# Two-layer cross attention on one core: first loads moved to GpSimd's queue, softmax factors asked for one period later, weight sums spread over the first units

## The chip, the cores and the metric

One Trainium2 chip, one core of it. The metric is the device time of one execution in microseconds (us). An engine that computes is TensorE (PE; its weight loads are listed as PEld), VectorE (DVE), ScalarE (ACT) or GpSimd (POOL); SyncE (SP) issues DMAs. The DMAs that an engine issues stand in its instruction stream in order: when one has to wait for a semaphore, everything behind it on that engine waits too.

## The reference

Two attention layers, one after the other, on x (8 sequences of 100 positions, 640 wide, 20 heads of 32). The context has 722 tokens, 1024 wide: 77 text tokens and 645 others ("ip"). Text and ip have a softmax each.

```python
# layer 0, per sequence
q = x @ Wq.T
k, v       = text @ Wk.T, text @ Wv.T        # 77 tokens
k_ip, v_ip = ip @ Wk_ip.T, ip @ Wv_ip.T      # 645 tokens
x = (softmax(q k^T / sqrt(32)) v + softmax(q k_ip^T / sqrt(32)) v_ip) @ Wo.T + bo + x
# layer 1: the same with other weights, but
#   ip scores get an addend shared by the heads, 0.5 * sem, where
#   sem = (softmax(q k_text^T * scale over all channels) @ text) @ ip^T * scale
#   ip probabilities are multiplied by a mask over the 100 positions
```

## The kernel before, in words

All arithmetic is fp32. The work has three stages.

**First stage, to about 215 us.** Text products, sums of weight quarters, and q of layer 0. The large products of ip with the weights are made by a twice nested scheme of seven products for eight, so weights and activations are first added and subtracted: among others by `text_differences` (L1012, on VectorE; its instructions are L1018 and L1022), `operand_sums` (L895) and `last_operands` (L931) on GpSimd, which also stores the results to scratch memory in DRAM (`op_d`, `os_d`, `ol_d`, `tx_d`).

**First two units, to about 545 us.** `made` (L1069) is the list of the tasks of production units 0 and 1 (k and v of the first sequences). While it runs, the sums that later weights need are put between its tasks: `place(at, each, parts)` puts part i behind task at + each*i. The buffers of this stage come from a pool of its own; pools of the next stage (k, v, tail, p, one) lie in the same memory, so the first load into a tile of theirs has to wait until what lay there is done with. Among that are the operands that `last_operands` stores: L948 adds, L949 is the store (ol_d<-olv, issued by GpSimd).

**Main loop, to the end.** 80 "products" (u, c): 16 units u (8 sequences in each of two layers) by 5 column chunks c of four heads. In period n the loop makes the scores of product n, and finishes product n-1 (`last`):

| place in the period | what is asked for |
|---|---|
| start | scores(n, part 0): 512 tokens, into the two score banks sc0, sc1 (L1310 on) |
| 0 to 0.4 | tasks of production and small pieces (`between`) |
| then | transposes(n-1, j=0, 1) |
| 0.4 to 0.6 | tasks |
| then | transposes(n-1, j=2, 3), directly followed by scores(n, part 1): the last 133 ip tokens and the text, into the same two banks |
| 0.6 to 0.8 | tasks (from n = 74 on these come behind the next line) |
| then | transposes(n-1, j=4, 5) |
| 0.8 to 1.0 | tasks |
| end | values(n-1), the product with v |

Layer 0 is n = 0 to 39, layer 1 n = 40 to 79. Transposes (L1432) go to a bank and are copied out to `pt`, by ScalarE for j = 0, 2, 4, 5 (L1440), by VectorE for j = 1, 3 (L1442).

**Softmax steps and the list `later`.** `scores` asks for the first pair of maxima at once and puts the rest on the list `later`, each with a mark that says whether it reads the score banks: maxima(1), exponentials(0), exponentials(1); for part 1 also text maxima and differences, text exponentials, then `factors` (VectorE, L1365: L1367 to L1371) and `widened`, `scaled_rest` (GpSimd L1377; ScalarE L1388; VectorE L1383). In layer 0 the maxima (L1321) and the exponentials (L1335) read the banks. In layer 1 one VectorE instruction per head (L1327) writes scores plus addend to `p` in on-chip memory and takes the extreme; the exponentials then read `p`, not the bank. Text exponentials are L1357 (layer 1, one for four heads) and L1360 (layer 0). `next_task` takes one entry off `later` whenever at least 1.0 us of task time has gone by; `free_scores` (L1296) asks for all entries up to the last one with the mark; `emit(len(later))` for all. The transposes j = 4, 5 need `scaled_rest` and `wide`; values need all copies.

**What sets the order.** Instructions of TensorE, VectorE and ScalarE run in exactly the order in which the program asks for them (`tc.manual_schedule(engines=PINNED)`, L1571). SP's and GpSimd's are placed by a scheduler. Streamed weights (`w`, six buffers) are loaded ahead by `take` on SP (L329, L348). The loads of the attention (`load_q` L1103, `load_vt` L1109, `load_k` L1116, `load_v` L1124, `load_res` L1144) are all on SP.

Of the kernel before, what the change touches and what calls it, by code (L numbers as in the profile page):

```python
# [14 lines left out]
P = 128  # L15
# [4 lines left out]
NT = 77  # L20
NI = 645
NL = NI - 5 * P
# [21 lines left out]
ORDER = [(u, c) for u in range(NU - 2) for c in range(NC_)]  # L44
# [5 lines left out]
def two_layer_xattn(  # L50
# [681 lines left out]
    with ExitStack() as es:  # L732
# [306 lines left out]
        with tc.manual_schedule(engines=PINNED):  # L1039
            text_sums()  # L1040
            all_of(weight_sums("k", 2 * P))
            fifth_sums()
            text_k(0)
            load_wk(wkt[1])
            left_v(0)
            all_of(operand_sums("v", 0))
            v = weight_sums("v", HC)
            all_of(v[:2])
            load_operands("k", 0, nc.gpsimd)
            text_v(0)  # L1050
            all_of(v[2:])
            all_of(operand_sums("k", 0))
            text_v_blocks(0)
            load_wv(wvt[1])
            all_of(weight_sums("k", 2 * P))
            load_operands("v", 1, nc.gpsimd)
            text_k(1)
            for h in range(2):
                load_a(0, 0, h)
            v = weight_sums("v", HC)  # L1060
            all_of(v[:2])
            text_v(1)
            all_of(v[2:])
            text_v_blocks(1)
            all_of(operand_sums("v", 1))
            for h in range(2):
                load_a(0, 1, h)
            left_text()
            made = lapped(unit_tasks(0, nc.vector) + unit_tasks(1, nc.vector))  # L1069
            made.pop(0)[1]()  # L1070
            for kc in range(HK):
                outer_piece(0, 5, kc)
            for which in (5, 6, 7, 3):
                inner_sum(0, OUTER[0], which, nc.vector)
            aside = {}

            def place(at, each, parts):
                for i, g in enumerate(parts):
                    aside.setdefault(at + each * i, []).append(g)

            place(100, 1, [lambda: load_operands("k", 1, nc.gpsimd)])
            place(40, 6, text_differences())
            place(270, 10, last_operands())
            for x, (_, f) in enumerate(made):
                f()
                if x == 110:
                    place(120, 18, operand_sums("k", 1))
                all_of(aside.get(x, []))

    banks[:] = [(ps_b, "b")]  # L1090
# [12 lines left out]
    def load_q(u):  # L1103
        l, b = divmod(u, B)
        t = tpool.tile([P, NC_, S], F32, tag="q", name=f"q_{u}")
        nc.sync.dma_start(t, q_d[l][b // 2][:, b % 2])
        qs_[u] = t

    def load_vt(u):  # L1109
        l, b = divmod(u, B)  # L1110
        t = tpool.tile([NTAIL, C], F32, tag="vt", name=f"vt_{u}")
        nc.sync.dma_start(t[:NL], vl_d[l][b * NL : (b + 1) * NL, :])
        nc.sync.dma_start(t[NL:], vt_d[l][b * NT : (b + 1) * NT, :])
        vts[u] = t

    def load_k(u, c):  # L1116

        l, b = divmod(u, B)
        t = kpool.tile([P, NK], F32, tag="k", name=f"k_{u}_{c}")
        nc.sync.dma_start(t[:, :NI], k_d[u][:, c, :])  # L1120
        nc.sync.dma_start(t[:, NI:], kt_d[l][c][:, b * NT : (b + 1) * NT])
        ks[u, c] = t

    def load_v(u, c):  # L1124
        t = vpool.tile([P, NB, P], F32, tag="v", name=f"v_{u}_{c}")
        nc.sync.dma_start(t, v_d[u].rearrange("(j p) n -> p j n", p=P)[:, :, c * P : (c + 1) * P])
        vs[u, c] = t

    def load_sem(u):
# [162 lines left out]
    def emit(n):  # L1292
        for _ in range(n):
            later.pop(0)[1]()

    def free_scores():  # L1296

        emit(max([i + 1 for i, (r, _) in enumerate(later) if r], default=0))

    def scores(u, c, part):  # L1300
        k0, k1 = ((0, KA), (KA, NK))[part]
        if part == 0:
            pr[u, c] = ppool.tile([S, 4, NK], F32, tag="p", name=f"p_{u}_{c}")

            stats[u, c] = stat.tile([S, 11, 4], F32, tag="st", name=f"st_{u}_{c}")
        else:
            free_scores()

        scs = [ps_sc.tile([P, 2, 512], F32, tag=f"sc{h}", name=f"sc_{u}_{c}_{part}_{h}") for h in range(2)]
        for i in range(4):  # L1310
            rows = slice(32 * i, 32 * i + 32)
# [109 lines left out]

    def transposes(u, c, j, at_end=False):
        if j == 0:
            emit(len(later))
            pts[u, c] = one.tile([P, 6, 4 * S], F32, tag="pt", name=f"pt_{u}_{c}")
        rows = P if j < 5 else NTAIL
        if at_end and j in (2, 3):
            ps = ps_sc.tile([P, 2, 512], F32, tag=f"sc{j - 2}", name=f"pspt_{u}_{c}_{j}")[:, 0]
        else:
            ps = ps_b.tile([P, 512], F32, tag="b", name=f"pspt_{u}_{c}_{j}")  # L1430
        for i in range(4):
            nc.tensor.transpose(  # L1432
                ps[:rows, i * S : (i + 1) * S], pr[u, c][:, i, j * P : j * P + rows], ident[:S, :S]
            )
        dst, src = pts[u, c][:rows, j, :], ps[:rows, : 4 * S]
        if j == 5:
            nc.tensor.transpose(ps[:, 4 * S : 5 * S], wide[u, c], ident[:S, :S])
            nc.scalar.copy(heads_sum(u, c), ps[:, 4 * S : 5 * S])
        if j in (0, 2, 4, 5):
            nc.scalar.copy(dst, src)  # L1440
        else:
            nc.vector.tensor_copy(dst, src)  # L1442
# [128 lines left out]
    with tc.manual_schedule(engines=PINNED):  # L1571
        todo = production()
        load_q(0)
        load_vt(0)
        load_k(0, 0)
        done = [0]
        since = [0.0]

        def next_task():

            if todo[done[0]][0]:
                if later and since[0] >= 1.0:
                    emit(1)
                    since[0] = 0.0
                since[0] += todo[done[0]][0]
            todo[done[0]][2]()
            done[0] += 1

        def make(until):
            while done[0] < len(todo) and todo[done[0]][1] < until:  # L1590
                next_task()

        mark = [0]

        def apart(until):

            while done[0] < len(todo) and todo[done[0]][1] < until and 1.7 > sum(
                t for t, _, _ in todo[mark[0] : done[0]]
            ):
                next_task()  # L1600
            while held_banks[0] > 1 and done[0] < len(todo) and todo[done[0]][1] < until + 0.1:
                next_task()
            mark[0] = done[0]

        def between(n, a, b, small):

            mark[0] = done[0]
            near = 0.7 if n < NC_ * LAST[0] + 2 else 0.1
            for i, (_, f) in enumerate(small):
                make(n + a + (b - a) * (i + 1) / (len(small) + 1))  # L1610
                apart(n + b + near)
                f()
            make(n + b)
            apart(n + b + near)

        make(0.0)
        last = None
        for n, (u, c) in enumerate(ORDER):
            at = small_work(n)
            loads(n)  # L1620
            scores(u, c, 0)
            if n == len(ORDER) - 1:
                load_v(*last)
                load_v(u, c)
            between(n, 0.0, 0.4, at[0])
            if last:
                transposes(*last, 0)
                transposes(*last, 1)
            between(n, 0.4, 0.6, at[1])
            if last:  # L1630
                transposes(*last, 2)
                transposes(*last, 3)
            scores(u, c, 1)
            if n == NC_ * LAST[0] - 1:
                load_q(LAST[1])
            few = n >= NC_ * LAST[0] + 4
            if not few:
                between(n, 0.6, 0.8, at[2])
            if n < len(ORDER) - 2:
                load_v(u, c)  # L1640
            if n + 1 < len(ORDER):
                load_k(*ORDER[n + 1])
            if last:
                transposes(*last, 4)
                transposes(*last, 5)
            if few:
                between(n, 0.6, 0.8, at[2])
            between(n, 0.8, 1.0, at[3])

            emit(len(later) - (n == len(ORDER) - 1))  # L1650
            if last:
                values(*last)
            emit(len(later))
            last = (u, c)
        last_out(0, [NC_ - 1])
        for j in range(6):
            transposes(*last, j, at_end=True)
        last_out_add(0)
        values(*last)
        last_out(1, [NC_ - 1])  # L1660
        last_out_add(1)
# [46 lines left out]
```

## Time and profile before

| | |
|---|---|
| runs | 2091.28, 2091.79, 2104.17 us; median 2091.79 |
| profiled execution, its own time | 2102.3 us |
| its span, first to last instruction | 2100.5 us |
| mean granted TensorE clock | 0.979 |
| VectorE, ScalarE, GpSimd busy | 59%, 39%, 50% |
| instructions | 43283 |
| a layer 0 period | about 22 us |
| a layer 1 period | about 16.6 us; the last ten 10 to 12 us |

How to read it. The page lists busy times per engine, then the span in 40 slices of 52.5 us with a digit for tenths. "PEclk" is the TensorE clock that was granted, in tenths of full speed. A group row gives line, engine, operation, output<-input with shapes, count, busy us, mean ns of one, then idle time ahead of it and what ended that. A wait row reads "engine tile line <- what it waited for: us in total, times, longest". A timeline row is start (us), duration, engine, line, operation; in brackets the idle time ahead of it and its cause. A window row is the window, its length, busy us and counts of PE, PEld, DVE, ACT, POOL, then granted clock, DMA share and GB/s. SPq is SP's queue of DMAs.

### The profile page before, as it was taken

Reading aid. Unit: us, or ns where it says so; the run is one execution under the profiler, and the core shown is the slowest. Engines: PE = TensorE matmul, PEld = TensorE weight load, DVE = VectorE, ACT = ScalarE, POOL = GpSimd, SP = SyncE. Lnnn points to the kernel's source line nnn. Section 1 sums busy time; section 2 is a strip of 40 time slices with the busy share of each in tenths; the row PEclk is TensorE's granted clock in tenths of the full one; section 3 lists DMA queues with packets and bytes.
Section 4 is the critical chain, followed back from the end, with each engine's and each line's share of the span. In section 5 each row is a group of like instructions: output and inputs, shape, how many; then the busy total and the mean of one; then the engine's idle time right before and its main releaser. Section 6 shows DMA issues by size and latency. Waiting matters only on the chain. (4 is left out here: it accounts for less than half of the span.)

```text
span 2100.5 us, 43283 instructions
## 1 busy us (share of the span) xinstructions
PE 1971.8 (94%) x15422; PEld 1608.4 (77%) x15422; DVE 1231.7 (59%) x3047; ACT 829.0 (39%) x2839; POOL 1039.9 (50%) x1256
## 2 busy tenths in 40 slices
PE   9999876899999999999999999999999999999998
PEld 8676765787777788778788888887877777676787
DVE  2322673554655754665457666657676666766666
ACT  1001000010244443544354435445554555556665
POOL 2788887545456452644445674663455355210110
PEclk9999998999999999999999999999999999999999
DMA  9577887777666667766776676666766666554441
GB/s 350 204 264 262 263 278 231 199 215 213 201 183 197 201 178 205 212 189 181 204 226 197 205 216 205 202 204 177 211 187 200 178 200 194 149 159 119 137 132 53
DMA packets 439600, 419.13 MB, mean 200 GB/s; under 512 B 67691, under 2 KB 381819, under 8 KB 439131
## 3 DMA queue, kind: packets, MB, share of 16 engines
q1 hardware_dynamic: 407982, 306.67, 50.7%
q0 software_dynamic: 26400, 101.03, 13.4%
q10 hardware_dynamic: 5004, 8.68, 1.1%
q8 instruction: 124, 2.03, 0.4%
q14 instruction: 90, 0.73, 0.1%
HBM read 315.07 MB, written 101.18 MB: 198 GB/s over the span
## 5 line engine op out<-in xcount | busy, mean ns | idle before, releaser
L441 POOL TENSOR_TENSOR cv<-cv,cv 128x320 f32<-128x320 f32 x252 | 219.7, 897 | 305.0 <-DVE cv L179 280.3
L1440 ACT COPY pt<-pspt 128x400 f32<-128x400 f32 x320 | 156.1, 491 | 226.2 <-PE pspt L1432 225.5
L441 POOL TENSOR_TENSOR ck<-ck,ck 128x256 f32<-128x256 f32 (+1 forms) x252 | 201.0, 803 | 67.9 <-DVE ck L179 44.4
L1432 PE MATMUL pspt<-ident,p 100*128 100x100 f32 (+1 forms) x1920 | 210.1, 252 | 19.3 <-ACT pt L1440 7.1
L1432 PEld LDWEIGHTS pspt<-ident,p 100*128 100x128 f32 (+1 forms) x1920 | 189.4, 139 | 50.5 <-issue 14.9
L1335 ACT ACTIVATE p<-sc,st 100x512 f32<-100x512 f32 (+1 forms) x320 | 166.6, 533 | 71.5 <-DVE st L1342 49.2
L1335 ACT ACTIVATE p<-p,st 100x512 f32<-100x512 f32 (+1 forms) x320 | 177.1, 557 | 11.7 <-DVE st L1327 9.3
L1377 POOL COPY wide<-st 100x128 f32<-100x128 f32 x80 | 30.4, 380 | 292.8 <-DVE st L1371 265.2
L479 PE MATMUL psv_d<-w,i 128*128 128x160 f32 (+1 forms) x1008 | 170.0, 312 | 3.2 <-DMA w<-text_t 1.0
L479 PEld LDWEIGHTS psv_d<-w,i 128*128 128x128 f32 x1008 | 154.3, 193 | 14.8 <-issue 3.0
L176 ACT COPY cv<-psv_a 128x320 f32<-128x320 f32 x126 | 53.7, 426 | 262.6 <-PE psv_a L479 241.7
L1312 PE MATMUL sc<-k,q 32*100 32x210 f32 (+1 forms) x1280 | 149.2, 507 | 8.2 <-ACT p L1360 7.0
L176 ACT COPY ck<-psk_a 128x256 f32<-128x256 f32 (+1 forms) x126 | 47.2, 374 | 256.9 <-PE psk_a L525 209.1
L1388 ACT ACTIVATE p<-p,st 100x133 f32<-100x133 f32 x316 | 102.3, 395 | 115.5 <-DVE st L1371 115.4
L525 PE MATMUL psk_d<-i,w 128*128 128x256 f32 (+1 forms) x504 | 134.6, 390 | 10.6 <-DMA w<-op_dk 6.0
L1327 DVE CUSTOM_DVE_ANT_0 p<-sc,sem 100x512 f32<-100x512 f32 (+1 forms) x320 | 139.5, 489 | 1.3 <-PE sc L1312 1.3
L1442 DVE COPY pt<-pspt 128x400 f32<-128x400 f32 x160 | 91.6, 573 | 73.6 <-PE pspt L1432 72.7
L1321 DVE TENSOR_REDUCE st<-sc 100x2 f32<-100x1024 f32 (+1 forms) x160 | 126.6, 824 | 7.7 <-PE sc L1312 7.3
L525 PEld LDWEIGHTS psk_d<-i,w 128*128 128x128 f32 x504 | 92.5, 192 | 37.4 <-issue 16.2
L479 PE MATMUL psv_a<-w,a 128*128 128x160 f32 (+1 forms) x576 | 107.1, 330 | 5.2 <-DVE ck L179 5.0
L179 DVE TENSOR_TENSOR cv<-psv_d,cv 128x320 f32<-128x320 f32 x126 | 61.6, 489 | 82.0 <-PE psv_d L479 80.7
L479 PEld LDWEIGHTS psv_a<-w,a 128*128 128x128 f32 x576 | 93.7, 196 | 12.3 <-DVE ck L179 5.3
(278 smaller groups left out, 4409.6 us busy)
## 6 DMA issues: line engine op xcount, KB each, us to landing
w<-op_dv SPq DMA_DIRECT2D x252, 160.0 KB
a<-ip_t SPq DMA_DIRECT2D x33, 1024.0 KB
w<-op_dk SPq DMA_DIRECT2D x252, 128.0 KB
k<-k_d SPq DMA_DIRECT2D x80, 322.5 KB
v<-v_d SPq DMA_DIRECT2D x80, 320.0 KB
v_d<-cv POOLq DMA_DIRECT2D x28, 640.0 KB, 4.9
w<-os_dv SPq DMA_DIRECT2D x108, 160.0 KB
k_d<-ck POOLq DMA_DIRECT2D x28, 512.0 KB, 4.5
```

Source lines behind the costliest of these rows:

```text
L176: nc.scalar.copy(c11, flat(bank))
L441: nc.gpsimd.tensor_tensor(to[:, a, b], of[:, a, b], other[:, a, b], ALU.add)
L479: nc.tensor.matmul(ps[:, o * pitch : o * pitch + m], lhsT=of[:, kc, o * w : o * w + P], rhs=wt[:, kc, :], start=(o == 0 and kc == 0 and no ...
L525: nc.tensor.matmul(ps[:, : 2 * w], lhsT=wt[:, kc, :], rhs=of[:, kc, :], start=(kc == 0 and not go_on), stop=(kc == 1), skip_group_check=True,)
L1312: nc.tensor.matmul(scs[i // 2][:S, i % 2, : k1 - k0], lhsT=qs_[u][rows, c, :], rhs=ks[u, c][rows, k0:k1], start=True, stop=True)
L1321: nc.vector.tensor_reduce(st[:, part, 2 * h : 2 * h + 2], scs[h][:S, :, :n], AX.X, ALU.max, negate=True)
L1327: nc.vector.tensor_tensor_reduce(out=p[:, i, k0 : k0 + n], in0=scs[h][:S, i % 2, :n], in1=sems[u][:, k0 : k0 + n], scale=-1.0, scalar=3.0e ...
L1335: nc.scalar.activation(dst, dst if l else scs[h][:S, i % 2, :n], AF.Exp, bias=st[:, part, i : i + 1], scale=-1.0 if l else 1.0, accum_out= ...
L1388: nc.scalar.activation(p[:, i, KA:NI], p[:, i, KA:NI], AF.Copy, scale=mul[:, 1, i : i + 1])
L1432: nc.tensor.transpose(ps[:rows, i * S : (i + 1) * S], pr[u, c][:, i, j * P : j * P + rows], ident[:S, :S])
L1440: nc.scalar.copy(dst, src)
L1442: nc.vector.tensor_copy(dst, src)
```

## The change

Four edits. First, in the first two units `load_operands` for k of layer 1, the text differences, the last operands and the operand sums of k are placed at other tasks, for two of them at numbers that follow from the length of `made`. Second, q and vt of units 0 and 1, and k and v of unit 0's first two chunks, are loaded by GpSimd's queue instead of SP's. Third, `scores` calls `free_scores` for part 0 too, and `transposes` no longer asks for all of `later` at j = 0. Fourth, the end of a period asks only for what reads the score banks (in the last period, as before), so that factors and scaling of a product are left on the list for the next period.

```diff
-            place(100, 1, [lambda: load_operands("k", 1, nc.gpsimd)])
-            place(40, 6, text_differences())
-            place(270, 10, last_operands())
+            place(46, 1, [lambda: load_operands("k", 1, nc.gpsimd)])
+            place(16, 6, text_differences())
+            place(len(made) * 3 // 4, 8, last_operands())
             for x, (_, f) in enumerate(made):
                 f()
-                if x == 110:
-                    place(120, 18, operand_sums("k", 1))
+                if x == 50:
+                    place(60, (len(made) * 3 // 4 - 60) // 7, operand_sums("k", 1))
                 all_of(aside.get(x, []))
...
     def load_q(u):
...
-        nc.sync.dma_start(t, q_d[l][b // 2][:, b % 2])
+        queue = nc.gpsimd if u < 2 else nc.sync
+        queue.dma_start(t, q_d[l][b // 2][:, b % 2])
...
     def load_vt(u):
...
-        nc.sync.dma_start(t[:NL], vl_d[l][b * NL : (b + 1) * NL, :])
-        nc.sync.dma_start(t[NL:], vt_d[l][b * NT : (b + 1) * NT, :])
+        queue = nc.gpsimd if u < 2 else nc.sync
+        queue.dma_start(t[:NL], vl_d[l][b * NL : (b + 1) * NL, :])
+        queue.dma_start(t[NL:], vt_d[l][b * NT : (b + 1) * NT, :])
...
     def load_k(u, c):
...
-        nc.sync.dma_start(t[:, :NI], k_d[u][:, c, :])
-        nc.sync.dma_start(t[:, NI:], kt_d[l][c][:, b * NT : (b + 1) * NT])
+        queue = nc.sync if u or c > 1 else nc.gpsimd
+        queue.dma_start(t[:, :NI], k_d[u][:, c, :])
+        queue.dma_start(t[:, NI:], kt_d[l][c][:, b * NT : (b + 1) * NT])
...
     def load_v(u, c):
...
-        nc.sync.dma_start(t, v_d[u].rearrange("(j p) n -> p j n", p=P)[:, :, c * P : (c + 1) * P])
+        queue = nc.sync if u or c > 1 else nc.gpsimd
+        queue.dma_start(t, v_d[u].rearrange("(j p) n -> p j n", p=P)[:, :, c * P : (c + 1) * P])
...
     def scores(u, c, part):
...
             stats[u, c] = stat.tile([S, 11, 4], F32, tag="st", name=f"st_{u}_{c}")
-        else:
-            free_scores()
-
+        free_scores()
...
     def transposes(u, c, j, at_end=False):
         if j == 0:
-            emit(len(later))
             pts[u, c] = one.tile([P, 6, 4 * S], F32, tag="pt", name=f"pt_{u}_{c}")
...
-            emit(len(later) - (n == len(ORDER) - 1))
+            if n == len(ORDER) - 1:
+                emit(len(later) - 1)
+            else:
+                free_scores()
             if last:
                 values(*last)
-            emit(len(later))
+            if n == len(ORDER) - 1:
+                emit(len(later))
             last = (u, c)
```

## The prediction, made before the changed kernel ran

> **What bounds the kernel now.** I read the page's busy times first, then TensorE's waits and granted clock, then the groups kept apart by shape, then single periods of the timeline.
>
> ```profile
> PE 1971.8 (94%) x15422; PEld 1608.4 (77%) x15422; DVE 1231.7 (59%) x3047; ACT 829.0 (39%) x2839; POOL 1039.9 (50%) x1256
> PE   9999876899999999999999999999999999999998
> PEclk9999998999999999999999999999999999999999
> ```
>
> TensorE is busy 94% of the span, evenly but for slices 5 to 7 (about 210 to 370 us). A change can win little more than its idle time; it loses each microsecond that TensorE is kept waiting, so the question is who waits for whom after the new order. TensorE's waits, whole span:
>
> ```profile
> PE psv_e L479 <- DMA w<-op_dv: 22.5, 6, 15.2
> PE psv_a L479 <- DVE ck L179: 7.4, 5, 2.5
> PE pspt L1432 <- ACT pt L1440: 7.1, 8, 1.4
> PE sc L1312 <- ACT p L1360: 7.0, 5, 2.1
> ```
>
> The columns are total, times, longest. One wait of 15.2 us stands out (326.9 to 342.1 us). The rest are short: after 1434 us, where layer 1 begins, they sum to about 41 us. The score matmuls (sc), which need the two score banks free, wait next to nothing. Why not is seen in a layer 1 period:
>
> ```profile
> 1870.95 0.56 PE L1432 MATMUL pspt<-ident,p 100*128 100x100 f32 x4 [0.55 <-ACT pt L1440]
> 1871.06 0.49 ACT L1440 COPY pt<-pspt 128x400 f32<-128x400 f32 x1
> 1871.44 0.61 PE L1312 MATMUL sc<-k,q 32*100 32x210 f32 x8
> 1871.55 0.57 DVE L1442 COPY pt<-pspt 128x400 f32<-128x400 f32 x1 [1.77 <-PE pspt L1432]
> ```
>
> Scores part 1 start at 1871.44, directly behind transposes j=3: the readers of part 0 (maxima; in layer 0 exponentials too) finished long before, because the old program asks for all of `later` ahead of transposes j=0. VectorE's copy of j=3 ends at 1872.12, 0.69 after the scores began (1871.55+0.57-1871.44); ScalarE's copy of j=2 ends 0.11 after they began (1871.06+0.49-1871.44; in a layer 0 period at 713 us 0.26).
>
> **What the order of the changed program, built, says.** TensorE's order is the same. ACT and DVE run the same instructions in another order, pinned. With the emission at transposes j=0 gone, what tasks do not trickle out one per microsecond is forced out by `free_scores` directly ahead of scores part 1, thus behind the copies of j=2 (ACT) and j=3 (DVE). Counting over the 80 periods:
> - Layer 0, part 0's exponentials behind the j=2 copy: all four in 5 periods (in two of them maxima(1) too behind the j=3 copy), the last two in 6.
> - Layer 1, maxima(1) of part 0 behind the j=3 copy: in 21 periods with factors (L1367 to L1371) and L1383 of the product before in between, in 3 with L1383 alone, in 9 with only the copy, in 7 not.
>
> Scores part 1 use the same banks, so TensorE waits in these 44 periods.
>
> **Durations** (groups by shape):
>
> ```profile
> L1335 ACT ACTIVATE p<-sc,st 100x512 f32<-100x512 f32 x160 | 108.6, 690 | 22.0 <-DVE st L1321 22.0
> L1388 ACT ACTIVATE p<-p,st 100x133 f32<-100x133 f32 x316 | 102.3, 395 | 115.5 <-DVE st L1371 115.4
> L1327 DVE CUSTOM_DVE_ANT_0 p<-sc,sem 100x512 f32<-100x512 f32 x160 | 101.4, 684 | 0.6 <-PE sc L1312 0.6
> L1383 DVE TENSOR_TENSOR p<-p,st 100x308 f32<-100x308 f32 x80 | 41.8, 522 | 0.0
> ```
>
> They overlap a little; by pitch in the timeline an exponential takes 0.73 us, a pair of L1327 1.30, L1367 to L1371 with L1383 1.63 (L1383 0.47 of it beside its neighbour).
>
> **Emission, layer 0.** Four exponentials: 0.11 to 0.26 + 4 x 0.73, about 2.95 us (3.2 where maxima(1) are late too); two: about 1.5. Sum 2 x 3.2 + 3 x 2.95 + 6 x 1.5 = 24.3 us.
>
> **Emission, layer 1.** Copy ends at +0.69, then 1.63, then 1.30, 0.06 from the end of the read until TensorE goes on (as in the rows of 1995 us below); the second pair of score matmuls, which needs it, would have come 0.26 after the first: 0.69+1.63+1.30+0.06-0.26 = 3.42. With L1383 alone about 2.18, with neither 1.79. Sum 21 x 3.42 + 3 x 2.18 + 9 x 1.79 = 94.4. One period pays part of it already:
>
> ```profile
> 1995.44 0.60 PE L1312 MATMUL sc<-k,q 32*100 32x210 f32 x4 [0.54 <-DVE st L1327]
> 1996.66 0.60 PE L1312 MATMUL sc<-k,q 32*100 32x210 f32 x4 [0.62 <-DVE st L1327]
> ```
>
> There maxima(1) happen to be late and TensorE waits 1.2 us for them: the mechanism in the trace of before. 94.4 - 1.2 = 93.2.
>
> **The end.** From product 74 no task lies between scores part 1 and transposes 4. L1388 (four, 1.30) and part 0's exponentials (2.9) then stand on ScalarE ahead of copies 4 and 5, which the value matmuls need: about 1.5 us in each of 6 periods, 9; in three periods the previous text exponentials stand there as well, 1 us each. 12 us. Earlier in layer 1 the tasks behind part 1 cover the same (2 to 4 us of matmuls); without that cover it would be another 27 x 1.5 = 40.
>
> **The clock.** After the short wait above:
>
> ```profile
> 1992.26:1998.50 6.24, 5.08 (x44) 3.48 (x41) 6.10 (x27) 4.99 (x14) 0.41 (x1) 0.94 1.05 309
> 1997.70:2001.10 3.40, 3.40 (x19) 3.40 (x19) 2.06 (x14) 0.80 (x3) 0.00 (x0) 0.50 1.17 294
> ```
>
> The granted clock (third column from the end) is 0.50 for 3.4 us behind it. After 540 us the trace has 16 TensorE gaps of 1.6 us or more; 11 are followed by half clock, 47.8 us in all, 3.0 us per gap, so 1.5 us lost per gap. 44 x 1.5 = 66 us. Bounds: 0, and 6.8 us of half clock per gap (the longest after 540), 3.4 lost, 150.
>
> The Trainium skill, "TensorE: Matmul & The Clock Gate", section "HAM oscillation", speaks of idle gaps of more than about 3.4 us as what costs the clock; by that only the 21 longest could, some 32 us instead of 66. The trace has half clock after gaps of 1.63 to 2.5 us, so the measurement decides.
>
> **What comes back.** Of the 41 us of waits in layer 1 the other engines' lateness (DVE adds, copies) is caught up while TensorE waits: 25 taken, with 10 for their half clock (bounds 0, and 41 + 15). Layer 0's score waits of 7.0 us (for ACT's text exponentials at the period's end) shrink by 3. VectorE no longer stands at L1367:
>
> ```profile
> DVE st L1367 <- ACT p L1357: 44.9, 34, 3.9
> ```
>
> That is VectorE's time, not TensorE's, and its 59% share does not need it; it is contained in the 25.
>
> **The start.** SP stood 15.5 us at the first q load (L1106), whose memory needs the last store of ol_d, issued by GpSimd at 332.67. Behind it on SP was the weight load that TensorE waited for:
>
> ```profile
> SPq L1106 <- DMA ol_d<-olv: 15.5, 1, 15.5
> ```
>
> The 12 moved DMAs leave SP for GpSimd's queue. But in the built order load_res(0) (L1155) takes q's place on SP and waits for the same store. So the stall is only shortened, by as much as GpSimd reaches that store earlier: its last sums are asked for sooner, which drops waits of 4.6, 1.8 and 1.4 and one add of 0.8 ahead of it, while about 3.5 us of new waits appear: 5 us (bounds 0, and 15.2 + 6.8 for its half clock). GpSimd pays 12 issues at 0.54 to 0.80 us, 6.5 to 9.6 us, and the landing waits of v and k (1 and 5 us); it is idle 334 to 345 us, which hides them, and four cv tiles lie between it and TensorE. Uncovered they would cost at most the same 10 to 16 us once. The text differences (13.7 us of VectorE, L1018 and L1022, from 261 to 295 us) come some 30 us earlier, where VectorE is busy 48 of 65 us and TensorE waits little for it; I take 0, with 13.7 each way as bounds, the most that the block can delay or release. GpSimd's operand sums for k move likewise; TensorE's waits for those weights (w from op_dk, os_dk and o_d) sum to some 18 us from 215 to 545 us, the bound of a gain; a loss of the same size if GpSimd, busy 46 of 65 us there, comes as late elsewhere; again 0. The Trainium skill, "DMA: Bandwidth & Descriptors", section "Issuing engines are not separate DMA queues", says that spreading issues over engines saves issue time alone; no run here shows it.
>
> **Sum.** 24.3 + 93.2 + 12 = 129.5; clock +66; back -(25+10+3) and -5: +152. The profiled execution took 2102.3 us (span 2100.5), 10.5 above the median of 2091.8; added to the median: 2244 us.
>
> **Rivals.**
> - Stalls as counted, but the clock hardly falls and everything in layer 1 is caught up: 129.5 - 41 - 5 = +84, 2175. For it: 5 of 16 gaps cost no clock. Against: 11 did.
> - The clock falls harder, 3.4 us per gap: 129.5 + 150 - 43 = +236, 2328. For it: layer 1's periods are 16.6 us, so gaps come close together; against: after 540 us only three half-clock stretches of 6.8 us exist.
> - Faster: VectorE, freed from L1367's 44.9 us, is early at the adds that TensorE waits for (psv_a, psk_d and pspt on DVE, some 29 us in all) and their clock (10): -39, with the start -5: 2048. It decides only if fewer than about 8 periods (39 / (3.42 + 1.5)) have the late maxima; the built order has 33 in layer 1.
> - The change does not do what it says: SP's stall stays, as another load takes its place. Price 5 us of the sum, never its sign.
>
> **How the numbers follow.** Forecast 0.57; milder clock 0.22; harder clock 0.13; faster 0.05; within 1% (about what a measurement of this kernel can tell from no change) 0.03. The range takes the forecast and most of the two beside it: 2150 (milder, with half the end hidden, -6, and the start giving 22 instead of 5, -17: 2152) to 2310 (3 us lost per gap: 129.5 + 132 - 43 = +218). Slower by over 1%: 0.57+0.22+0.13 = 0.92.
>
> **What would show it.** PE sc L1312 <- DVE st L1327 at some 90 us over 30 or more times, and <- ACT p L1335 at some 20; PEclk digits of 8 and 9 in place of 9 in layer 1, half-clock stretches of 3.4 us behind the waits; L1367's wait for L1357 nearly gone; psv_e's wait for op_dv still about 10 us, SP waiting at L1155. Wrong if sc's waits stay under 40 us, or if TensorE's other waits vanish by more than 40.

## The result, and the profile after

| | before | after |
|---|---|---|
| median | 2093.36 us (4 runs, 2091.28 to 2104.17) | 2269.18 us (4 runs, 2265.14 to 2270.11) |
| ratio | | 1.0825, 95% interval 1.0785 to 1.0865 |
| span of the profiled execution | 2100.5 us | 2263.4 us |
| granted clock, mean | 0.979 | 0.947 |

The change makes the kernel 8% slower. Forecast were 2244 us, +152 on the median; measured are +176 between medians and +163 between the profiled executions. The page of the changed kernel first:

```profile
PE 2061.5 (91%) x15422; PEld 1668.8 (74%) x15422; DVE 1246.1 (55%) x3047; ACT 824.3 (36%) x2839; POOL 1040.2 (46%) x1268
PE   9999769989999998999999989999898998888887
PEclk9999989999999999999999999999898998888888
```

TensorE has the same 15422 instructions and is busy 89.7 us longer. Some 72 us of that is the clock: half of the time in which TensorE worked at half clock, a half that is 107.1 us after and 35.2 before. But for one in slice 6, the 8s among the clock's digits stand from slice 29 on, where layer 1 runs. Most of the rest is seen in the matmuls of scores part 1, before and after:

```profile
L1312 PE MATMUL sc<-k,q 32*100 32x210 f32 x640 | 51.1, 382 | 1.2 <-DVE st L1327 1.2
L1314 PE MATMUL sc<-k,q 32*100 32x210 f32 x640 | 85.2, 409 | 109.4 <-DVE st L1329 89.0 <-ACT p L1337 20.1
```

One of them takes 409 ns in place of 382, but together they keep TensorE busy 85.2 us in place of 51.1. All eight of a product overlap when they come together (0.61 us for x8 in the prediction's row at 1871.44); when a wait splits them, four alone take as long (0.60 us for x4 in the row at 2174.92 below).

The other 73 us of the span are idle time of TensorE. Its waits (total, times, longest) say for whom:

```profile
PE sc L1314 <- DVE st L1329: 89.0, 34, 3.8
PE sc L1314 <- ACT p L1337: 20.1, 18, 1.8
PE psv_e L479 <- DMA w<-op_dv: 12.2, 3, 8.0
PE psf L554 <- DMA w<-wki: 7.5, 5, 4.3
PE psk_d L525 <- DVE ck L179: 7.3, 4, 3.7
PE psk_a L525 <- DMA w<-os_dk: 7.1, 3, 3.3
PE sc L1314 <- ACT p L1362: 7.0, 5, 2.1
```

(L1329 and L1337 are L1327 and L1335 of before: the lines are 1 to 4 further on.) The scores, which waited 1.2 us for VectorE's maxima before, wait 89.0 us. One of these waits, in the timeline of the changed kernel:

```profile
2174.41 1.19 DVE L1443 COPY pt<-pspt 128x400 f32<-128x400 f32 x2 [0.33 <-PE pspt L1433]
2174.92 0.60 PE L1314 MATMUL sc<-k,q 32*100 32x210 f32 x4
2175.57 0.47 DVE L1369 TENSOR_REDUCE st<-p 100x4 f32<-100x308 f32 x1
...
2176.73 0.47 DVE L1385 TENSOR_TENSOR p<-p,st 100x308 f32<-100x308 f32 x1
...
2177.12 0.68 DVE L1329 CUSTOM_DVE_ANT_0 p<-sc,sem 100x512 f32<-100x512 f32 x1
...
2177.73 0.69 DVE L1329 CUSTOM_DVE_ANT_0 p<-sc,sem 100x512 f32<-100x512 f32 x1
...
2178.48 1.02 PE L1314 MATMUL sc<-k,q 32*100 32x210 f32 x4 [2.96 <-DVE st L1329]
```

VectorE copies transposes 1 and 3, then makes the factors of the product before, and only then reads the second score bank, which the second half of scores part 1 needs. Nothing of this is more work; it is the same work in an order that has TensorE's need last. The window rows of layer 1 up to product 73 and of the last six periods, first before, then after (granted clock is the third column from the end):

```profile
1445.20:2017.30 572.10, 536.48 (x5035) 429.09 (x5027) 384.39 (x1309) 316.21 (x1024) 195.91 (x236) 0.98 0.59 174
2017.30:2100.50 83.20, 74.37 (x898) 64.11 (x891) 54.74 (x213) 53.41 (x177) 7.84 (x14) 0.96 0.26 72
```

```profile
1477.70:2148.50 670.80, 589.54 (x5033) 467.70 (x5029) 398.50 (x1309) 316.44 (x1024) 195.95 (x236) 0.91 0.50 148
2148.50:2263.40 114.90, 89.79 (x895) 73.25 (x891) 55.85 (x213) 52.91 (x177) 7.86 (x14) 0.82 0.18 52
```

By stages, from the first score matmuls of a product to those of the next stage in the two traces ("clock lost" is half of the time at half clock in the stage):

| stage | before | after | more | more idle on TensorE | clock lost, before and after |
|---|---|---|---|---|---|
| to product 0 | 551.2 | 545.3 | -5.9 | -8.4 | 18.8, 17.1 |
| layer 0 | 894.0 | 932.4 | +38.4 | +19.6 | 10.2, 22.2 |
| layer 1, to product 73 | 572.1 | 670.8 | +98.7 | +45.6 | 11.9, 59.7 |
| the last six periods | 83.2 | 114.9 | +31.7 | +16.3 | 3.6, 20.6 |

### The profile page after: what moved, and what is told of

It reads as the page before. It is cut to its first block, busy times and chain, and to the rows that moved or that the text cites. A ratio compares the mean times of both kernels' runs of the same rounds, so it can differ in the third digit from the quotient of the medians.

```text
span 2263.4 us, 43383 instructions
## 1 busy us (share of the span) xinstructions
PE 2061.5 (91%) x15422; PEld 1668.8 (74%) x15422; DVE 1246.1 (55%) x3047; ACT 824.3 (36%) x2839; POOL 1040.2 (46%) x1268
## 5 line engine op out<-in xcount | busy, mean ns | idle before, releaser
L1314 PE MATMUL sc<-k,q 32*100 32x210 f32 (+1 forms) x1280 | 185.6, 532 | 116.3 <-DVE st L1329 89.0
L1433 PEld LDWEIGHTS pspt<-ident,p 100*128 100x128 f32 (+1 forms) x1920 | 199.3, 144 | 40.8 <-issue 20.4
L1433 PE MATMUL pspt<-ident,p 100*128 100x100 f32 (+1 forms) x1920 | 219.8, 259 | 6.7 <-DVE ck L179 5.7
L1337 ACT ACTIVATE p<-sc,st 100x512 f32<-100x512 f32 (+1 forms) x320 | 166.6, 533 | 49.8 <-DVE st L1344 43.5
L1314 PEld LDWEIGHTS sc<-k,q 32*100 32x100 f32 x1280 | 61.0, 169 | 159.5 <-DVE st L1329 101.0
L1337 ACT ACTIVATE p<-p,st 100x512 f32<-100x512 f32 (+1 forms) x320 | 176.5, 556 | 3.4 <-DVE st L1329 3.3
L479 PEld LDWEIGHTS psv_d<-w,i 128*128 128x128 f32 x1008 | 156.2, 195 | 16.3 <-issue 3.0
L1329 DVE CUSTOM_DVE_ANT_0 p<-sc,sem 100x512 f32<-100x512 f32 (+1 forms) x320 | 141.6, 489 | 33.3 <-PE sc L1314 33.2
```

Source lines behind the costliest of these rows:

```text
L479: nc.tensor.matmul(ps[:, o * pitch : o * pitch + m], lhsT=of[:, kc, o * w : o * w + P], rhs=wt[:, kc, :], start=(o == 0 and kc == 0 and no ...
L1314: nc.tensor.matmul(scs[i // 2][:S, i % 2, : k1 - k0], lhsT=qs_[u][rows, c, :], rhs=ks[u, c][rows, k0:k1], start=True, stop=True)
L1329: nc.vector.tensor_tensor_reduce(out=p[:, i, k0 : k0 + n], in0=scs[h][:S, i % 2, :n], in1=sems[u][:, k0 : k0 + n], scale=-1.0, scalar=3.0e ...
L1337: nc.scalar.activation(dst, dst if l else scs[h][:S, i % 2, :n], AF.Exp, bias=st[:, part, i : i + 1], scale=-1.0 if l else 1.0, accum_out= ...
L1433: nc.tensor.transpose(ps[:rows, i * S : (i + 1) * S], pr[u, c][:, i, j * P : j * P + rows], ident[:S, :S])
```

## The experiments

**The theory** (A): late readers of the score banks keep TensorE waiting, and the clock falls behind the waits. The rivals: the loads and the moved sums cost the time (B); the late factors and scaling cost it by themselves (C, G); the clock is low for another reason (E).

**Emission alone.** The kernel before with the third and fourth edit.

> The kernel before with the third and fourth edit alone (what is asked for when); loads and weight sums as before. Theory A (late readers of the score banks make TensorE wait, and the clock falls behind the waits): nearly the whole loss, 2265 to 2280 us, scores waiting about 89 us for maxima (the layer 1 instruction on VectorE) and about 20 us for exponentials. Rival B (the loads on GpSimd's queue and the moved sums cost time as well): under 2240, the rest being theirs.

Measured: 2263.43 us against 2092.86, ratio 1.0788 (1.0747 to 1.0828). The two score rows are those of the changed kernel, 89.0 and 20.1 us, to the tenth. The median lies 1.6 us under the expected band; the loss is all there, and B falls.

**The start alone.** The changed kernel with the old emission.

> The changed kernel with the emission of before: loads on GpSimd's queue and spread sums alone. Theory A: 2082 to 2092 us, since the first stage ended 6 us earlier in the changed kernel (551.2 to 545.3 us) and nothing later reads it. Rival B: over 2100.

Measured: 2092.31 us, ratio 0.9999 (0.998 to 1.0017). No loss, but no gain either: it lies 0.3 us above the band that A expected. SP still stands before the same store, now at the residual's load, and TensorE still waits at the same weight:

```profile
SPq L1159 <- DMA ol_d<-olv: 8.6, 1, 8.6
```

```profile
PE psv_e L479 <- DMA w<-op_dv: 15.4, 3, 12.3
```

**Bank readers first.** Factors still come a period later, but the readers of the banks are taken out of the list ahead of them.

```diff
+    def readers_only():
+        for e in [e for e in later if e[0]]:
+            later.remove(e)
+            e[1]()
...
     def scores(u, c, part):
...
-        free_scores()
+        (emit(len(later)) if part else free_scores())
...
     def transposes(u, c, j, at_end=False):
         if j == 0:
+            readers_only()
```

> The changed kernel, except that at transposes j=0 the entries that read the score banks are asked for, out of their order, and all that is left at scores part 1. Factors and scaling still come a period later. Theory A: the score waits are gone (under 10 us), clock back near 0.98, 2075 to 2100 us. Rival C (what costs is that factors and scaling come late: transposes 4 and 5 and the values wait for them): the time stays over 2200 us, with TensorE waiting at pspt and pv instead.

Measured: 2140.73 us, ratio 1.0208 (1.0172 to 1.0244): between the two. The waits for the maxima are gone (0.6 us are left). Most of what remains is C's, in one place: in the last six periods (114.0 us, against 83.3 with the start alone) TensorE waits at the transposes for the late scaling. The waits in those periods:

```profile
PE pspt L1439 <- ACT p L1395: 15.5, 6, 3.2
PE pspt L1439 <- ACT pt L1447: 2.1, 2, 1.2
```

Layer 1 up to product 73 takes 577.0 us, 3.9 more than with the start alone. There tasks lie between scores part 1 and transposes 4, and TensorE waits for the scaling only 5.7 us in 34 periods. Layer 0 takes 907.4 us, 19.3 more than with the start alone; why stays open.

**The same, with the old emission from product 73 on.** The edit, against the run before:

```diff
     def transposes(u, c, j, at_end=False):
         if j == 0:
-            readers_only()
+            (emit(len(later)) if ORDER.index((u, c)) >= 73 else readers_only())
...
+            elif n >= 73:
+                emit(len(later))
             else:
                 free_scores()
```

> The kernel that asks for the bank readers first, with the emission of before from product 73 on, where no task lies between scores part 1 and transposes 4. If its loss of 48 us sits there (TensorE waited 15.5 us at transposes for the late scaling in the last six periods, which took 31 us longer than before), 2105 to 2115 us; if the loss is spread over the loop, within 10 us of 2141.

Measured: 2108.93 us, ratio 1.0091 (1.0064 to 1.0119); the last six periods take 81.9 us. So 32 of the 48 us were the end's. Of the rest some 13 us stand in layer 0 (901.6 against 888.1 with the start alone), and were not followed further.

**Each of the two emission edits by itself.** First the one at j=0 (the period's end as before):

> The changed kernel with the end of a period as before (all is asked for there); only the emission at transposes j=0 is gone. Theory A, refined: the leftover factors fill the head of the list, so that the maxima behind them are not reached by the tasks. Without leftovers the order has late maxima in 3 periods in place of 33: 2095 to 2115 us (3 waits, and the last six periods with exponentials ahead of copies 4 and 5, 5 to 10 us). Rival F (the missing emission at j=0 is enough by itself): over 2200 us.

Measured: 2081.87 us, ratio 0.9958 (0.9934 to 0.9982). Better than expected: not a loss but a gain. Layer 1 up to product 73 takes 561.6 us, against 573.1 with the start alone. There TensorE no longer waits at transposes for copies (5.9 us for ScalarE's and 3.1 for VectorE's with the start alone, 0.2 now), which fits that copies 0 and 1 no longer stand behind a block of maxima and exponentials. F falls. Then the edit at the period's end, with j=0 kept:

> The changed kernel with the emission at transposes j=0 kept; only the end of a period leaves factors and scaling to the next one. Theory A, refined: no maxima behind copies, so 2085 to 2105 us. Rival G (leaving factors to the next period costs by itself): over 2120 us.

Measured: 2169.54 us, ratio 1.0378 (1.0355 to 1.0401). A's expectation failed and G's holds: leaving the factors over costs by itself, though no maxima stand behind copies. TensorE now waits for VectorE's copies themselves; before, the first of these rows had 5.0 us and the second did not occur:

```profile
PE pspt L1434 <- DVE pt L1444: 22.5, 19, 2.7
PE psv_a L479 <- DVE pt L1444: 15.2, 3, 6.0
```

Why is in the timeline of this kernel:

```profile
1546.38 0.46 DVE L1369 TENSOR_REDUCE st<-p 100x4 f32<-100x308 f32 x1
...
1549.06 0.46 DVE L1385 TENSOR_TENSOR p<-p,st 100x308 f32<-100x308 f32 x1
...
1549.45 0.68 DVE L1329 CUSTOM_DVE_ANT_0 p<-sc,sem 100x512 f32<-100x512 f32 x1
1550.06 0.68 DVE L1329 CUSTOM_DVE_ANT_0 p<-sc,sem 100x512 f32<-100x512 f32 x1
1550.67 0.56 DVE L1444 COPY pt<-pspt 128x400 f32<-128x400 f32 x1
...
1551.29 0.91 PE L1434 MATMUL pspt<-ident,p 100*128 100x100 f32 x8 [2.55 <-DVE pt L1444]
```

Factors and late maxima are one block of VectorE work (here 4.3 us, of which L1371 alone takes 1.22 us; its median is 0.16). Asked for at j=0 it stands ahead of copy 1, and the next transposes wait for their bank; asked for at scores part 1 it stands behind copy 3, and the scores wait. The block moves, and in these two places TensorE waits for it.

**The clock by itself.** 20 more transposes, whose results nobody reads, ahead of scores part 1 in the 21 periods with factors ahead of the maxima.

```diff
+            if n in (41, 42) or 60 <= n < 80 and n != 68:
+                for _ in range(20):
+                    nc.tensor.transpose(fill[0][:, 4 * S : 5 * S], pr[last][:, 0, : P], ident[:S, :S])
             scores(u, c, 1)
```

> The changed kernel with 20 more transposes (about 2.7 us of TensorE, results never read) ahead of scores part 1, in the 21 layer 1 periods in which factors stand ahead of the late maxima. TensorE works where it waited; the order on ACT and DVE is the same. Theory A, its clock part (half clock is paid for the idle gap): scores wait some 50 us less for the maxima, the clock rises, and the time falls by 30 to 55 us although nothing was taken away: 2215 to 2240 us. Rival E (the low clock has another cause, for instance what the other engines do, or it does not set the time there): within 10 us of 2269, or longer by part of the added work.

Measured: 2219.63 us against 2269.18 of the changed kernel (ratio to the kernel before 1.062, 1.0597 to 1.0642, where the changed kernel had 1.0825). TensorE does more and ends some 50 us earlier. Its waits for the maxima and the granted clock of the same two stages:

```profile
PE sc L1314 <- DVE st L1329: 33.7, 34, 3.6
```

```profile
1471.60:2109.00 637.40, 584.03 (x5331) 466.55 (x5327) 398.71 (x1309) 315.87 (x1024) 195.90 (x236) 0.97 0.52 156
2109.00:2215.90 106.90, 90.35 (x1017) 75.25 (x1011) 55.83 (x213) 52.96 (x177) 7.86 (x14) 0.95 0.20 56
```

0.91 has become 0.97 and 0.82 has become 0.95; after 540 us TensorE is at half clock for 87.1 us in place of 207.1, which is 60 us of time. Half clock is paid for the idle time, and E falls.

**A start that clears SP.** The start alone, with the loads that the scheduler would put in q's place on GpSimd's queue as well.

```diff
-            nc.sync.dma_start(t[:, :n], x_t[:, b : b + n])
+            queue = nc.sync if g else nc.gpsimd
+            queue.dma_start(t[:, :n], x_t[:, b : b + n])
```

(Likewise the first three tiles of output weights in load_wo, and load_sem and load_g of unit 8.)

> As the run with the start alone, and the further loads that the scheduler would put in q's place on SP (first residual, three output weights, the first text keys and text rows of layer 1) on GpSimd's queue too, so that SP waits for no memory of the first stage. Theory A's reading of the start (SP waits for the last store of the first stage's operands, whatever load stands there): psv_e's wait for op_dv of 8.0 us falls under 3 us, 2065 to 2085 us. Rival D (the weights that this wait holds back would be late anyway, or GpSimd's own work is delayed by the issues): no gain over the start alone, within 5 us.

Measured: 2085.19 us, ratio 0.9951 (0.9928 to 0.9974). The median lies 0.2 us above the band. SP waits for no store of ol_d any more. TensorE still waits 3.8 us at that place (up to 332.6 us; under 3 was expected) and then 3.0 us for another weight at 345 us: weights are late there for other reasons too. D falls, by 7 us against the start alone (the two intervals do not meet); the gain is a third of what the old wait of 15.2 us and its half clock might have given.

**A version that beats both.** The j=0 emission dropped up to product 72, everything else as before:

```diff
     def scores(u, c, part):
...
-        else:
-            free_scores()
-
+        free_scores()
...
     def transposes(u, c, j, at_end=False):
         if j == 0:
-            emit(len(later))
+            if ORDER.index((u, c)) >= 73:
+                emit(len(later))
```

> The kernel before, start and period end unchanged, with one edit: up to product 72 nothing is asked for at transposes j=0 (free_scores asks ahead of the scores instead). Theory A, refined by the run without j=0's emission (2082 us): the gain of that run is due to the exponentials and maxima no longer standing ahead of copies j=0 and j=1, so 2075 to 2085 us, its gain in layer 1. Rival H (that gain came from the start, the loads and sums): within 4 us of the kernel before.

Measured: 2082.86 us, ratio 0.995 (0.993 to 0.997); layer 1 up to product 73 takes 558.0 us, against 572.1 before. H falls. With the cleared start:

> The same edit together with the start in which GpSimd's queue also takes the first residual, the first three output weights and layer 1's first text loads (alone: 2085 us, 7.7 under before). If the two gains add, 2066 to 2076 us; if they overlap, 2077 to 2085 us.

Measured: 2072.37 us against 2095.01, ratio 0.9894 (0.9862 to 0.9926). The two gains add: 12.2 and 7.7 us alone, 22.6 together. This is the fastest kernel of the study.

## Why the prediction was right, point by point

- **Order and waits, layer 1**: right. Forecast 93.2 us in 33 periods; 89.0 us in 34 waits. The two are not quite the same measure. The forecast's 3.42 counts from where the second pair of score matmuls would have started, 0.26 us after the first; a wait counts from the end of the first pair, 0.60 us after its start. In the forecast's measure the wait shown above is 2.96 + 0.60 - 0.26 = 3.30, and the 34 waits are some 100 us. That a split pair also loses its overlap with the other is priced in the forecast only by this difference. (By the prediction's own terms its 2.18 would be 1.79 + 0.47 = 2.26, which is 0.2 us in the sum.)
- **Layer 0**: 24.3 us forecast, 20.1 measured (18 waits, since both banks can wait in a period). With the clock 24.3 + 11 x 1.5 - 3 = +38; measured +38.4. The agreement is in part luck: TensorE is idle 19.6 us longer and loses 12.0 us to the clock, and most of the rest is the score matmuls, which are busy 8.6 us longer there. The small term in the sum was wrong: the waits for ACT's text exponentials did not shrink by 3, they are 7.0 us in both kernels.
- **The clock**: the mechanism right, the term mis-sized. Forecast 66 us less 10 returned; measured 207.1 us at half clock after 540 us where it was 53.7, so (207.1 - 53.7) / 2 = 77 us. There are 40 gaps of 1.6 us and more, 16 before (forecast: 44 periods with waits), and 35 of them are followed by half clock. But each takes 207.1 / 40 = 5.2 us of it, where before it was 53.7 / 16 = 3.4 (4.7 against the forecast's 3.0, if only the stretches behind gaps are counted): half of the stretches are 6.8 us long, where before most were 3.4. The price was read off gaps of 2.7 us at most and put on waits of 3.42. It lies between the forecast and the rival with the harder clock. The rule weighed in the prediction (the Trainium skill, "TensorE: Matmul & The Clock Gate", section "HAM oscillation": idle gaps of more than about 3.4 us) is not what these traces show: the 40 gaps last 2.6 us on average and 3.8 at most, and 30 of the 35 that are shorter than 3.4 us are followed by half clock.
- **The end**: 12 us were counted twice. The likely reason: while TensorE waits for the late maxima, ScalarE gets through what stands ahead of copies 4 and 5: after the change TensorE waits 19.1 us for the maxima in those periods and 0.3 and 0.2 us at transposes and values. The term exists, but shows only when the score waits are taken away: 15.5 us in the run with the readers first. Forecast for the last six periods 6 x 3.42 + 12 + 6 x 1.5 = 41.5, measured 31.7.
- **What comes back**: 25 forecast. In layer 1 up to product 73 TensorE waits 69.9 us for the maxima, 68.7 more than before, and is idle only 45.6 us longer: 23.1 came back. (Layer 1's first scores are at 1445 us, not at 1434 as the prediction has it.)
- **VectorE's wait at L1367** (L1369 after): 44.9 us became 4.4, and TensorE got nothing for it, as forecast. The rival in which this decides is out.
- **The start**: 5 us forecast, the stage ended 5.9 us earlier, TensorE's wait 8.0 in place of 15.2 us. One execution says little here: over all traces that wait is 15.1 to 19.4 us in the three with the old start and 5.9 to 17.4 us, 10.3 on average, in the seven with the new one. So the forecast's 5 us show on average at that place, but in the time of the start alone they do not (0.998 to 1.0017). That SP's stall stays, because another load takes its place, was right.
- **Sum**: by stages -5.9 + 38.4 + 98.7 + 31.7 = +162.9 between the profiled executions. By kind they are 73.2 of idle time, 71.9 of clock while TensorE works, and 17.8 of busy time beyond that, near what the score matmuls lose by being split. The forecast's +152 is 56 of clock and 129.5 - 28 - 5 = 96.5 of all else, where 73.2 + 17.8 = 91.0 were measured. That the second part fits so well is in part luck: the end's 12 us counted twice and the lost overlap, which was not fully priced, offset each other. What is short is the clock.

What the prediction did not see is that the two emission edits have to be told apart: it spoke of the missing emission at j=0, which alone is a gain of 0.4%. The entries left over from the period before alone cost some 78 us. Together the two cost more, about 177 us: the entries left over stand at the head of the list, the tasks reach them first, and with no emission at j=0 the maxima behind them are forced out only at scores part 1.

## What to carry to other kernels

Work that is put off does not vanish from an in-order engine: ask which instruction of the bounding engine waits behind the place to which it moves, in each stage, and above all where the covering work is gone. When a list is emptied first in, first out, what is left over on it delays what is put on it next, so ask by need (who holds a bank that the next step wants), not by age. And a wait of 2 to 4 us on TensorE can cost more than its length: after 540 us the 40 gaps of this kernel are 105 us of idle time, and the half clock costs 104 us more.

## What the runs showed of the hardware that was not expected

- Longer idle gaps were followed by more half clock. In the changed kernel 25 gaps are 2.7 us or longer: all are followed by half clock, 5.6 us each. The other 15 have 3.2 us each, as in the kernel before, where all 16 are shorter and have 3.0. Dummy matmuls in the gaps gained 50 us. The long gaps are also those that come close together (14 to 21 us apart at the end), so whether the length or the distance makes the difference is not shown.
- A VectorE instruction that was priced at its pitch is at times long beside GpSimd's. The row of L1385 in the changed kernel (shortest, median and longest in ns):

```profile
L1385 DVE TENSOR_TENSOR p<-p,st x80: 461/471/4378, 565.5 to 2252.7; 100x308 f32<-100x308 f32 x80
```

In the trace, 25 of the 80 have a tensor_tensor of GpSimd beside them and take 1215 ns on average; the 55 others take 474 ns, 565 at most. In the kernel before it was 19 with 682 ns (2159 at most) and 61 with 473. No run changes this alone, so the cause is not shown. In the changed kernel this stretch is ahead of the maxima; in the forecast it was priced at its pitch without GpSimd.
